# Three moves in a one-core graph network kernel: a late adjacency row, half of the turned features, and the queue of three outputs

## The chip, the core and the metric

The kernel runs on one core of one Trainium2 chip. The metric is the device time of one execution in microseconds. Before the change the median of three runs is 699.59 us (699.44 to 699.65).

The engines are called as in the profile: PE is TensorE (matmul), PEld its weight load, DVE is VectorE, ACT is ScalarE, POOL is GpSimd, SP is SyncE. SP, ACT and POOL also issue DMAs, each from a queue of its own that runs in program order.

## The reference

The input is `x` (3327 nodes, 64 features) and a symmetric-pattern, sparse adjacency matrix `adj` (3327 x 3327, f32, stored dense). Four layers, each with a layer norm and a relu in front and a residual (`x = x + layer(relu(norm(x)))`):

```python
# layer 0: twice h = relu(ggc(h, adj, ...)), a gated cell
m = adj @ (x @ W); gi = m @ wih.T + bih; gh = x @ whh.T + bhh
r, z = sigmoid(i_r + h_r), sigmoid(i_z + h_z); n = tanh(i_n + r * h_n)
h = (1 - z) * n + z * x
# layer 1: each row's last 100 neighbours, weighted by powers of 1/2
mask = adj != 0; rank = cumsum(mask, axis=1); k = min(deg, 100)
w = mask * where(rank > deg - k, 0.5 ** (deg - rank), 0); out = w @ (input @ weight) + bias
# layer 2: three times x = (adj * adj) @ x @ W.T + b
# layer 3: twice x = tanh(concat([adj @ x, x]) @ W)
```

So `adj` (or something made from it) is multiplied with a feature matrix eight times, one after the other.

## The kernel before, in words

**Tiles and stages.** The 3327 nodes are padded to 26 blocks of 128. The source nodes of a tile are one block q of 128; its columns are the target nodes of one of two groups. Group 0 has chunks 0 and 1 (3 and 3 blocks), group 1 has chunks 2 and 3 (3 and 4 blocks), each taken twice since two halves of the nodes (s = 0, 1) lie side by side. A tile is 128 x 2 x 768 f32 (group 0) or 128 x 2 x 896 (group 1), and is loaded by SP (L411) into one of 20 slots. The eight multiplications are numbered k = 0 to 7: 0 and 1 are layer 0, 2 is layer 1 ("ranked"), 3 to 5 are layer 2 ("squared": ACT, or DVE in part, squares the tile, L446 and L448), 6 and 7 are layer 3. A unit of work is (k, chunk, tile): two matmuls (L613), one for each s, into a PSUM bank that gathers the sums of a chunk over all 26 tiles. `alone` and `joint` list the units so that one loaded tile serves two multiplications of one group where it can. When a chunk's sums are complete, a task `after_k` turns them into the next features.

**The ranked stage.** A tile is first turned into a mask of ones and zeros (bf16). DVE compares with zero in two halves (L472), for 127 rows; the last row of the mask is not of the tile, but the count of neighbours that lie behind it, and comes by a small DMA on POOL's queue (L477) from `totals`. PE multiplies the mask with a triangle (L313), and ACT (L529) or DVE (L527) evicts the result with a relu as int16 bits, which read as bf16 are the powers of one half (`e`). PE multiplies those with the features (L613). A mask takes half a slot, called a room (class `Mask`). Since row 127 of every tile is left out, these "last sources" are gathered apart for each group by `last_sources(g)` (L564 to L583): POOL clears a room (L570), SP loads the rows 127 of all tiles into it (two DMAs, L574), DVE compares and scales (L576), subtracts the counts (L580), and ACT evicts (L582) into `lastw[g]`, which the last unit of the stage multiplies. The room is then free for a mask.

**Order.** The program is written out for each engine by hand; no scheduler changes the order. Tasks are Python generators: `yield us` says how much planned TensorE time must pass before the next step. `spend(us)` after each unit counts the planned time of that unit (0.86 us for a full unit) down for every task and runs those that are due. So the number in `later_task(200.0, ...)` and the yields inside a task decide where in each engine's program its instructions stand, and not when they run. `run` looks 44 units ahead for loads, 24 for masks, 3 for evictions; `mask_pieces` puts the halves of masks on DVE one or more at a time. `finish` runs the rest of a task at once, where its result is needed.

**What else the change touches.** `gru` (L874) is the gated cell of layer 0. Its sums are evicted into `both[c]`; ACT does the sigmoids (L890) and the tanh (L906), DVE the products (L895, L897, L910 to L912). For the first cell, the relu of one half of the features is made on DVE (L914, s = 1) and the other on ACT (L917, s = 0). Then `after_0` (L947) turns the features back to nodes on rows: for group 0 by matmuls with an identity, for group 1 by DVE's 32 x 32 transposes (L961), 8 for each s, into the tile that the matmuls of k = 1 read. `after_7` (L1029) is the end of the kernel for a chunk: sums evicted by ACT (L830) and DVE (L834), matmuls with the weights (L780), tanh on ACT (L1034), the residual on DVE (L1037), and the output by DMA on ACT's queue (L1039). Group 1's two chunks come out earlier; group 0 is last, with chunk 1 split into two parts (numbers 4 and 5), so that five outputs are issued in all.

Of the kernel before, what the change touches and what calls it, by code (L numbers as in the profile page):

```python
# [52 lines left out]
NC = 4  # L53
PARTS = (4, 5)
CWM = 512
GROUPS = [(0, 1), (2, 3)]
# [35 lines left out]
def upper(n):  # L92
    return slice(n * D, (n + 1) * D)
# [3 lines left out]
def kernel(  # L97
# [9 lines left out]
    nc = tc.nc  # L107
# [9 lines left out]
    xs = const.tile([P, NB, 2, D], F32, name="xs")  # L117
# [10 lines left out]
    both = [const.tile([P, 2, (b1 - b0) * P], F32, name=f"both{c}") for c, (b0, b1) in enumerate(CH[:NC])]  # L128
# [173 lines left out]
    def blocks(c):  # L302
        return CH[c][1] - CH[c][0]

    def width(c):
        return blocks(c) * P
# [15 lines left out]
    def take(sums=False, either=True):  # L322


        either = either and not sums
        pool = idle_sums if sums else idle_temps
        if either and idle_sums and (not pool or released[idle_sums[0]] < released[pool[0]]):
            pool = idle_sums
        for c in list(tasks):
            if not pool and c not in running:  # L330
                advance(c)
        i = pool.popleft()
        return i, banks[i]

    def give(i):
        released[i] = max(released) + 1
        (idle_sums if i < 4 else idle_temps).append(i)

    def nodes(c):

        return feat.tile([P, blocks(c), 2, D], F32, name=f"y{c}")

    def flat(t):
        return t.rearrange("p b s d -> p b (s d)")
# [4 lines left out]
    def xchunk(c):  # L349
        return xs[:, CH[c][0]:CH[c][1]]  # L350

    def view(ps, c):
        return ps[:, :width(c)].rearrange("p (b f) -> p b f", f=P)
# [5 lines left out]
    def advance(c):  # L359
        running.add(c)  # L360
        try:
            tasks[c][1] = next(tasks[c][0])
        except StopIteration:
            del tasks[c]
        running.discard(c)

    def begin(c, task):
        finish(c)
        tasks[c] = [task, 0.0]
        advance(c)  # L370

    def finish(c):
        while c in tasks:
            advance(c)

    def later_task(us, task):
        yield us
        yield from task
# [185 lines left out]
    def last_sources(g):  # L564

        w = sum(width(c) for c in GROUPS[g])
        w0 = CH[GROUPS[g][0]][0] * P
        room = Mask(w)
        v = room.view.rearrange("p s w -> p (s w)").bitcast(F32)
        nc.gpsimd.memset(v, 0.0)  # L570
        yield 4.0
        rows = adjT.rearrange("(q p) (s n) -> q p s n", p=P, s=2)
        for s in range(2):
            nc.sync.dma_start(out=v[s * D:s * D + NQ], in_=rows[:, P - 1, s, w0:w0 + w])  # L574
        yield 12.0
        nc.vector.tensor_scalar(v, v, 0.0, 129.0 * TWO7, op0=ALU.not_equal, op1=ALU.mult)  # L576
        for c in GROUPS[g]:
            finish(("count", c))
        yield 1.0
        nc.vector.scalar_tensor_tensor(v, totals[g], -TWO7, v, op0=ALU.mult, op1=ALU.add)  # L580
        yield 1.5
        nc.scalar.activation(lastw[g], v, AF.Relu, bias=bitsb)  # L582
        room.free()  # L583
# [189 lines left out]
    def stacked_to_nodes(c, w):  # L773

        i, ps = take()
        v = view(ps, c)
        for b in range(blocks(c)):
            for s in range(2):
                for n in range(2):
                    nc.tensor.matmul(v[upper(n), b, upper(s)], both[c][:, s, b * P + n * D:b * P + (n + 1) * D], w(s),  # L780
                                     start=True, stop=True)
        return i, v
# [46 lines left out]
    def evacuate_stacked(acc, c, on_scalar=False):  # L829
        nc.scalar.copy(both[c][upper(0), 0], acc[0][1][upper(0), :width(c)])  # L830
        if on_scalar:
            nc.scalar.copy(both[c][upper(1), 1], acc[1][1][upper(1), :width(c)])
        else:
            nc.vector.tensor_copy(both[c][upper(1), 1], acc[1][1][upper(1), :width(c)])  # L834
        for i in {acc[0][0], acc[1][0]}:
            give(i)
# [31 lines left out]
    def add_row(c, i):  # L868
# [2 lines left out]
        nc.vector.tensor_tensor(groups(xchunk(c)), groups(xchunk(c)),  # L871
                                brow[:, i:i + 1, :].to_broadcast([P, n, D]), ALU.add)

    def gru(acc, c, bi, bh, cell, pace=1.0):  # L874

        w = width(c)
        evacuate_stacked(acc, c, on_scalar=cell == 0)
        yield 0.8 * pace
        at = dead.popleft()
        r, z, d = (slots[at].rearrange("p s w -> p (s w)")[:, i * CWM:i * CWM + w] for i in range(3))  # L880

        def gate(g):
            i, ps = take()
            for s in range(2):
                nc.tensor.matmul(ps[upper(1 - s), :w], cells[:, cell, s, g, :], both[c][:, s], start=True, stop=True)  # L885
            return i, ps

        for g, v in enumerate((r, z)):
            i, ps = gate(g)
            nc.scalar.activation(v, ps[:, :w], AF.Sigmoid, bias=bsum[:, cell, g:g + 1])  # L890
            give(i)
        nh = None if cell == 0 else gate(2)
        ni = gate(3)
        yield 1.0 * pace
        nc.vector.scalar_tensor_tensor(r, ahead[c] if nh is None else nh[1][:, :w], bcol[:, bh + 2:bh + 3], r,  # L895
                                       op0=ALU.add, op1=ALU.mult)
        nc.vector.tensor_tensor(r, r, ni[1][:, :w], ALU.add)  # L897
        give(ni[0])
        if nh is not None:
            give(nh[0])  # L900
        else:
            del ahead[c]
            if not any(ch in ahead for ch in GROUPS[c // 2]):
                rooms[c // 2].free()
        yield 1.0 * pace
        nc.scalar.activation(r, r, AF.Tanh, bias=bcol[:, bi + 2:bi + 3])  # L906
        yield 0.8 * pace
        for s in range(2):
            u = upper(1 - s)
            nc.vector.tensor_tensor(d[u], both[c][u, s], r[u], ALU.subtract)  # L910
        nc.vector.tensor_tensor(d, d, z, ALU.mult)
        nc.vector.tensor_tensor(d, d, r, ALU.add)  # L912
        if cell == 0:
            nc.vector.tensor_scalar(both[c][upper(0), 1], d[upper(0)], 0.0, None, op0=ALU.max)  # L914
        yield 2.4 * pace
        if cell == 0:
            nc.scalar.activation(both[c][upper(1), 0], d[upper(1)], AF.Relu)  # L917
            yield 1.0 * pace
        return at, d
# [27 lines left out]
    def after_0(c, acc):  # L947
        at, _ = yield from gru(acc, c, BI1, BH1, 0)
        dead.append(at)
        yk = nodes(c)  # L950
        if c in GROUPS[0]:
            i, v = stacked_to_nodes(c, lambda s: ident[:, upper(1 - s)])
            yield 0.8
            nc.vector.tensor_copy(flat(yk), v)
            give(i)
        else:
            for s in range(2):
                v = both[c][upper(1 - s), s].rearrange("p (b q n) -> p b q n", q=4, n=32)
                for f in range(2):
                    for q in range(4):  # L960
                        nc.vector.transpose(yk[q * 32:(q + 1) * 32, :, s, f * 32:(f + 1) * 32],  # L961
                                            v[f * 32:(f + 1) * 32, :, q])
                    yield 0.6
        y[1][c] = yk

    def after_1(c, acc):
        pace = 1.0 if c in GROUPS[0] else 1.2
        at, h2T = yield from gru(acc, c, BI2, BH2, 1, pace)
        v = transpose_to_nodes(h2T, c)
        dead.append(at)  # L970
        yield 0.8 * pace
        residual(v, c, relu=True)
        yk = nodes(c)
        yield from layernorm_relu(yk, c, TWO27, 1.2 * pace, squares_on_scalar=c in GROUPS[1])
        y[2][c] = yield from in_three(yk, c)
        yield 80.0 if c in GROUPS[1] else 14.0
        add_row(c, 3)
# [51 lines left out]
    def after_7(c, acc):  # L1029
        evacuate_stacked(acc, c)  # L1030
        yield 1.3
        v = stacked_to_nodes(c, lambda s: w3[:, 1, s])
        t = work.tile([P, 4, 2, D], F32, name="t2")[:, :blocks(c)]
        nc.scalar.activation(flat(t), v[1], AF.Tanh)  # L1034
        give(v[0])
        yield 0.8
        nc.vector.tensor_tensor(flat(xchunk(c)), flat(xchunk(c)), flat(t), ALU.add)  # L1037
        g0, g1 = CH[c]
        nc.scalar.dma_start(out=out[:, g0:g1], in_=xs[:, g0:g1])  # L1039

    after[:] = [after_0, after_1, after_2, after_3, after_4, after_5, after_6, after_7]

# [20 lines left out]
    begin(2, later_task(4.0, before_0(2)))  # L1063
    begin(3, later_task(10.0, before_0(3)))
    begin(NC + 1, later_task(130.0, last_sources(0)))
    begin(NC + 2, later_task(200.0, last_sources(1)))
    run()
    for c in list(tasks):
        finish(c)
# [39 lines left out]
```

## Time and profile before

| | before |
|---|---|
| runs, median (lowest to highest) | 699.59 us (699.44 to 699.65) |
| profiled execution | 699.51 us |
| its span on the core | 697.6 us |
| granted TensorE clock | 0.999 |
| PE busy | 680.2 us, 97% |
| DVE, ACT, POOL busy | 354.5, 274.4, 79.1 us |
| L613, the multiplications with f32 tiles | 535.5 us in 3016 matmuls |
| L961, transposes of layer 0 for group 1 | 9.1 us in 32 |
| L576, L580, L582, for both groups | 1.2, 2.0 and 2.0 us in 2 each |
| L1037, the last residuals | 2.5 us in 5 |

The profile's times are microseconds from the start of the span. A timeline row gives the start, the busy time, engine, line and operation, what is written `<-` what is read, the count of instructions in the row, and in brackets the idle time of the engine ahead of it with what ended it. `SPq`, `ACTq` and `POOLq` are the issue of DMAs on that engine. [...]

### The profile page before, as it was taken

Reading aid. Unit: us, or ns where it says so; the run is one execution under the profiler, and the core shown is the slowest. Engines: PE = TensorE matmul, PEld = TensorE weight load, DVE = VectorE, ACT = ScalarE, POOL = GpSimd, SP = SyncE. Lnnn points to the kernel's source line nnn. Section 1 sums busy time; section 2 is a strip of 40 time slices with the busy share of each in tenths; the row PEclk is TensorE's granted clock in tenths of the full one; section 3 lists DMA queues with packets and bytes.
Section 4 is the critical chain, followed back from the end, with each engine's and each line's share of the span. In section 5 each row is a group of like instructions: output and inputs, shape, how many; then the busy total and the mean of one; then the engine's idle time right before and its main releaser. Section 6 shows DMA issues by size and latency. Waiting matters only on the chain.

```text
span 697.6 us, 12581 instructions
## 1 busy us (share of the span) xinstructions
PE 680.2 (97%) x5072; PEld 377.9 (54%) x5072; DVE 354.5 (51%) x772; ACT 274.4 (39%) x426; POOL 79.1 (11%) x114
## 2 busy tenths in 40 slices
PE   6899999999999998999999999999999999999997
PEld 4686667635566785556444444333344444344586
DVE  5946745665997899747442107325271565005101
ACT  1013000403147878888998107722176500000101
POOL 5300000002390423111100000000000000000000
PEclk9999999999999999999999999999999999999999
DMA  9999998099879534783899569954998399918991
GB/s 339 401 401 406 405 406 268 3 359 377 268 246 369 212 126 153 267 276 121 288 382 330 203 222 408 405 217 141 394 367 269 105 402 405 405 59 285 403 403 45
DMA packets 68693, 201.31 MB, mean 289 GB/s; under 512 B 7244, under 2 KB 8372, under 8 KB 68636
## 3 DMA queue, kind: packets, MB, share of 16 engines
q1 hardware_dynamic: 65292, 198.69, 76.5%
q10 hardware_dynamic: 1168, 1.63, 0.7%
q8 instruction: 40, 0.66, 0.4%
q0 software_dynamic: 2176, 0.20, 0.2%
q14 instruction: 17, 0.14, 0.1%
HBM read 199.45 MB, written 0.85 MB: 287 GB/s over the span
## 4 chain that ended last, share of the span: by engine, by line
PE 86%; DVE 8%; DMA 3%; POOL 2%; issue 1%; ACT 1%; ACTq 0%; DVEq 0%; POOLq 0%
PE sum L613 73%; PE temp L313 5%; DMA adj<-in_adjT 2%; PE temp L548 2%; PE temp L885 2%; DVE adj L472 2%; PE sum L313 1%; PE sum L885 1%; PE temp L780 1%; DVE e L527 1%; DVE adj L910 1%; POOL both L251 1%; DVE y L961 1%; POOL st L854 1%; DVE st L851 1%
## 5 line engine op out<-in xcount | busy, mean ns | idle before, releaser
L613 PE MATMUL sum<-adj,y 128*64 128x384 f32 (+3 forms) x3016 | 535.5, 501 | 4.0 <-DVE y L858 1.4
L613 PEld LDWEIGHTS sum<-adj,y 128*64 128x64 f32 x3016 | 248.0, 137 | 233.8 <-issue 197.9
L446 ACT ACTIVATE adj<-adj 128x768 f32<-128x768 f32 (+1 forms) x176 | 144.3, 892 | 45.7 <-PE sum L613 21.9
L472 DVE TENSOR_SCALAR adj<-adj 128x768 bf16<-128x768 f32 (+3 forms) x208 | 113.4, 596 | 32.6 <-PE temp L548 24.7
L613 PE MATMUL sum<-e,both 128*64 128x384 bf16 (+1 forms) x624 | 73.9, 339 | 1.1 <-DVE e L527 1.1
L529 ACT ACTIVATE e<-temp,bitsb 128x384 int16<-128x384 f32 (+1 forms) x120 | 67.6, 608 | 14.7 <-PE temp L313 9.4
L830 ACT COPY both<-sum 64x384 f32<-64x384 f32 (+3 forms) x17 | 8.1, 478 | 149.0 <-PE sum L613 147.9
L854 POOL TENSOR_TENSOR st<-st,mhalf 128x6 f32<-128x6 f32 (+1 forms) x16 | 24.9, 1554 | 288.7 <-DVE st L852 288.7
L834 DVE COPY both<-sum 64x384 f32<-64x384 f32 (+3 forms) x13 | 7.2, 560 | 98.6 <-ACT both L830 98.6
L448 DVE TENSOR_TENSOR adj<-adj 128x768 f32<-128x768 f32 (+1 forms) x32 | 30.6, 1005 | 51.8 <-DMA adj<-in_adjT 33.1
L613 PEld LDWEIGHTS <-both 128*64 128x64 bf16 x624 | 41.2, 110 | 19.6 <-issue 7.0
L313 PE MATMUL temp<-adj,tri 128*64 128x384 bf16 (+1 forms) x332 | 51.4, 341 | 0.4 <-DVE e L527 0.2
L477 POOL DMA_DIRECT2D adj<-totals x52 | 34.8, 671 | 46.3 <-PE temp L313 32.4
L527 DVE TENSOR_SCALAR e<-temp 128x384 int16<-128x384 f32 (+1 forms) x46 | 28.3, 616 | 20.6 <-ACT e L529 10.9
L313 PEld LDWEIGHTS <-tri 128*64 128x64 bf16 x416 | 28.9, 110 | 16.1 <-issue 7.8
L809 DVE STREAM_TRANSPOSE both<-y 32x96 f32<-32x96 f32 (+1 forms) x128 | 35.6, 278 | 2.9
L548 PE MATMUL temp<-adj,behind 128*64 128x384 bf16 x208 | 33.8, 340 | 2.6 <-DVE adj L472 2.5
L825 DVE STREAM_TRANSPOSE y<-t 32x96 f32<-32x96 f32 (+1 forms) x64 | 17.8, 278 | 24.7 <-ACT t L816 23.9
L548 PEld LDWEIGHTS <-behind 128*64 128x64 bf16 x208 | 20.8, 110 | 17.2 <-issue 13.3
L761 DVE COPY t<-sum 128x384 f32<-128x384 f32 x6 | 3.3, 553 | 35.8 <-PE sum L613 35.8
L186 ACT COPY t<-temp 128x128 f32<-128x128 f32 x1 | 0.3, 266 | 48.2 <-PE temp L184 48.2
L570 POOL MEMSET adj<- 128x768 f32 (+1 forms) x2 | 1.6, 790 | 139.4 <-PE sum L613 133.9
(132 smaller groups left out, 352.0 us busy)
## 6 DMA issues: line engine op xcount, KB each, us to landing
adj<-in_adjT SPq DMA_DIRECT2D x130, 768.0 KB, 9.1
adj<-in_adjT SPq DMA_DIRECT2D x104, 896.0 KB, 11.6
xs<-in_x ACTq DMA_DIRECT2D x1, 448.0 KB
adj<-totals POOLq DMA_DIRECT2D x26, 3.0 KB, 4.9
adj<-totals POOLq DMA_DIRECT2D x26, 3.5 KB, 2.5
out<-xs ACTq DMA_DIRECT2D x2, 192.0 KB, 4.4
out<-xs ACTq DMA_DIRECT2D x1, 256.0 KB
xs<-in_x ACTq DMA_DIRECT2D x1, 192.0 KB, 3.4
```

Source lines behind the costliest of these rows:

```text
L313: nc.tensor.matmul(out[hs], lhsT[:, hs], rhs, start=start, stop=stop)
L446: nc.scalar.activation(sq, v, AF.Square)
L448: nc.vector.tensor_tensor(sq, v, v, ALU.mult)
L472: nc.vector.tensor_scalar(t.mask.view[:rows, half], t.view()[:rows, half], 0.0, None, op0=ALU.not_equal)
L477: nc.gpsimd.dma_start(out=t.mask.view[P - 1:P], in_=totals[t.g][t.q:t.q + D + 1:D, :])
L527: nc.vector.tensor_scalar(wide[:, s], ps[:, :w], BITS, 0.0, op0=ALU.add, op1=ALU.max)
L529: nc.scalar.activation(wide[:, s], ps[:, :w], AF.Relu, bias=bitsb)
L548: nc.tensor.matmul(counts[c][1][s * D:(s + 1) * D, :w], behind[:, NQ - 1 - t.q:NQ - 1 - t.q + D], t.mask.view[:, s, t.cols(c)], start=firs ...
L613: nc.tensor.matmul(acc[h][1][h * D:(h + 1) * D, :w], yq[h], rhs[h], start=first and n == 0, stop=last and n == len(terms) - 1)
L809: nc.vector.transpose(to[at:at + 32, :, q], h[q * 32:(q + 1) * 32, :, s, f * 32:(f + 1) * 32])
L854: nc.gpsimd.tensor_tensor(st[:, 3, :n], st[:, 2, :n], mhalf[:, :n], ALU.pow)
L885: nc.tensor.matmul(ps[upper(1 - s), :w], cells[:, cell, s, g, :], both[c][:, s], start=True, stop=True)
```

## The change

Three things are edited.

First, the transposes of group 1's features after k = 0. A helper `turn` makes the 8 transposes of one s. `gru` calls it for s = 1 right behind DVE's relu, before it yields; `after_0` calls it for s = 0 where all 16 stood, and the yields of 0.6 between them are gone.

Second, `last_sources(1)` begins after 240 us of planned time and not 200. In the program of the engines this puts POOL's L570 fifteen places further on in its queue, directly behind the mask row that is issued at 296.06 in the profile of before; SP's two L574 ten loads later; DVE's L576 and L580 and ACT's L582 close to the end of group 1's ranked stage. The rooms of the masks made in between are handed out in another order, and the last mask of the stage is made in the room that L582 frees. The order of PE's instructions is the same.

Third, the outputs of chunks 0 and 1 (three DMAs: chunk 0, parts 4 and 5) are issued on SP's queue. Those of group 1 stay on ACT's.

```diff
+    turned = {}
+
+    def turn(yk, c, s):
+
+        v = both[c][upper(1 - s), s].rearrange("p (b q n) -> p b q n", q=4, n=32)
+        for f in range(2):
+            for q in range(4):
+                nc.vector.transpose(yk[q * 32:(q + 1) * 32, :, s, f * 32:(f + 1) * 32], v[f * 32:(f + 1) * 32, :, q])
+
     def gru(acc, c, bi, bh, cell, pace=1.0):
...
             nc.vector.tensor_scalar(both[c][upper(0), 1], d[upper(0)], 0.0, None, op0=ALU.max)
+            if c in GROUPS[1]:
+                turned[c] = nodes(c)
+                turn(turned[c], c, 1)
         yield 2.4 * pace
...
     def after_0(c, acc):
         at, _ = yield from gru(acc, c, BI1, BH1, 0)
         dead.append(at)
-        yk = nodes(c)
         if c in GROUPS[0]:
+            yk = nodes(c)
...
         else:
-            for s in range(2):
-                v = both[c][upper(1 - s), s].rearrange("p (b q n) -> p b q n", q=4, n=32)
-                for f in range(2):
-                    for q in range(4):
-                        nc.vector.transpose(yk[q * 32:(q + 1) * 32, :, s, f * 32:(f + 1) * 32],
-                                            v[f * 32:(f + 1) * 32, :, q])
-                    yield 0.6
+            yk = turned.pop(c)
+            turn(yk, c, 0)
         y[1][c] = yk
...
-        nc.scalar.dma_start(out=out[:, g0:g1], in_=xs[:, g0:g1])
+        queue = nc.scalar if c in GROUPS[1] else nc.sync
+        queue.dma_start(out=out[:, g0:g1], in_=xs[:, g0:g1])
...
-    begin(NC + 2, later_task(200.0, last_sources(1)))
+    begin(NC + 2, later_task(240.0, last_sources(1)))
```

## Prediction, made before the changed kernel ran

> **What bounds the kernel now.** I first read the page's totals and its chain of waits.
>
> ```profile
> span 697.6 us, 12581 instructions
> PE 680.2 (97%) x5072; PEld 377.9 (54%) x5072; DVE 354.5 (51%) x772; ACT 274.4 (39%) x426; POOL 79.1 (11%) x114
> PE 86%; DVE 8%; DMA 3%; POOL 2%; issue 1%; ACT 1%; ACTq 0%; DVEq 0%; POOLq 0%
> ```
>
> TensorE is busy 680.2 of 697.6 us. The change takes no work from it, so a gain can only come out of the 17.4 us in which it stands. Next, the windows of 5 us (columns: wall, busy PE, PEld, DVE, ACT, POOL, clock, DMA share, GB/s) show where it stands near the edits.
>
> ```profile
> 145.00:150.00 5.00, 4.28 (x25) 1.61 (x24) 4.74 (x17) 0.00 (x0) 0.00 (x0) 1.00 0.81 278
> 270.00:275.00 5.00, 4.30 (x45) 2.82 (x43) 5.00 (x11) 4.85 (x8) 3.29 (x4) 1.00 0.26 45
> 275.00:280.00 5.00, 3.20 (x23) 1.41 (x21) 5.00 (x9) 3.99 (x5) 0.48 (x1) 1.00 0.43 166
> 315.00:320.00 5.00, 5.00 (x58) 3.17 (x56) 4.78 (x9) 4.62 (x9) 2.19 (x4) 1.00 0.05 14
> 690.00:695.00 5.00, 3.28 (x61) 2.87 (x55) 1.78 (x5) 1.78 (x5) 0.00 (x0) 1.00 0.14 46
> ```
>
> At 145 and at 270 to 280 PE waits while VectorE is full: there VectorE is the bound. At 315 to 320 PE is full, and VectorE and ScalarE nearly are. At 690 the chain of the outputs is all that is left. The timelines of these places give what ends each wait.
>
> [...] when DMA is idle: the mask rows of L477 land 1.6 us after issue at 317 to 320, but 5 us among loads (285.88 to 291.01); 6.4 is the longest. [...]
>
> **Part A, the turned features (L957 to L963).** The first 8 transposes of chunk 2 need only VectorE's own relu (s=1), the other 8 need ScalarE's (L917); now they stand in one block behind the latter.
>
> ```profile
> 132.79 0.35 DVE L914 TENSOR_SCALAR both<-adj 64x384 f32<-64x384 f32 x1
> 136.12 0.75 DVE L895 SCALAR_TENSOR_TENSOR adj<-adj,bcol,adj 128x512 f32<-128x512 f32 x1 [2.98 <-ACT adj L890]
> 138.38 2.25 DVE L961 STREAM_TRANSPOSE y<-both 32x96 f32<-32x96 f32 x8 [0.58 <-ACT both L917]
> 143.88 7.33 DVE L961 STREAM_TRANSPOSE y<-both 32x96 f32<-32x96 f32 x24
> 146.17 1.29 PE L613 MATMUL sum<-adj,y 128*64 128x384 f32 x6 [0.72 <-DVE y L961]
> ```
>
> Eight of width 96 take 2.25 us, and VectorE idles 2.98 us at 133.1. So the s=1 half of chunk 2 goes there for nothing (133.2 to 135.4, before L895 at 136.12). The s=0 half stays at 138.38. Behind 143.9 only chunk 3's 16 are left, 7.33 − 2.25 = 5.1 us, ending near 149.0. PE's matmuls on s=1 of chunk 2 then don't wait at 146.17. The half unit before starts at 144.83, and its successors follow each 0.43 us, so 145.26 was due: **0.9 us** gained (0.72 of it shown as idle). Next late is chunk 3's features: PE asks for them at 150.73 now, 149.8 then; 149.0 is 0.8 us early. Without the idle place the 2.25 us would come back at L895. Loads have 14 us or more of slack in this stage. Bounds: 0.7 to 1.0.
>
> **Part B, group 1's last sources (L564 to L583).** Seven instructions move: L570, two L574, L576, L580, L582 and the waits with them. First what they leave.
>
> ```profile
> 274.87 0.61 DVE L576 TENSOR_SCALAR adj<-adj 128x896 f32<-128x896 f32 x1
> 275.40 0.68 DVE L527 TENSOR_SCALAR e<-sum 128x512 int16<-128x512 f32 x1
> 276.00 1.15 DVE L472 TENSOR_SCALAR adj<-adj 127x896 bf16<-127x896 f32 x2
> 277.07 1.08 DVE L580 SCALAR_TENSOR_TENSOR adj<-totals,adj 128x896 f32<-128x896 bf16 x1
> 278.61 0.55 DVE L527 TENSOR_SCALAR e<-sum 128x384 int16<-128x384 f32 x1
> 279.21 1.08 PE L613 MATMUL sum<-adj,y 128*64 128x512 f32 x4 [1.19 <-DVE e L527]
> ```
>
> VectorE runs without a gap, and PE waits for L527. By starts, L576 takes 0.53 us of that row and L580 1.00. Without them the L527 at 278.61 is done at 277.63 and PE goes on at 277.68 instead of 279.21; its own work is ready at 277.15. **1.53 us** gained. ScalarE's L582 (1.04 us at 278.19) leaves as well, and counts nothing, since VectorE is the later one. Bounds: 1.2 (another wait takes the end of it) to 1.6.
>
> On SP and POOL:
>
> ```profile
> SPq L574 <- POOL adj L570: 23.2, 2, 22.0
> POOL adj L477 <- ACT lastw L582: 5.9, 1, 5.9
> ```
>
> SP stands 22.0 us (231.7 to 253.8) at L574 and the loads behind it land by 260; the first mask of them is made at 279.68. Unblocking them is worth nothing, as they are early already. At the new place L574 stands behind L570, and that behind the mask row of 296.06 on POOL: memset near 296.6, both L574 near 297.5 to 298.6 (0.54 each). The load behind them went out at 297.34: 1.3 us late, against 8 us between its landing (304.3) and its mask. Nothing.
>
> Now what they enter. By the order of instructions L576, one L472, one L527 and L580 stand among the last masks of group 1 (VectorE, 316 to 319), and L582 on ScalarE between evictions (L529) that run 13 in 6.42 us without a gap from 317.64, in the time of before at about 319.5. Two things follow.
> - The evictions behind L582 come 0.95 us later; they had 0.2 to 0.5 us in hand, so TensorE waits about 0.7 us.
> - The last mask is made in the half slot that L582 frees: its L472 and its row by DMA (L477, POOL) wait for L582, which ends at 320.58. Before, that room was free, and the last three rows were issued at 317.19 to 318.30, one behind the other. A row issued at 320.62 lands 1.6 us later as at 317.19, or 2.45 as the one that followed L582 before (279.52 to 281.97): 322.2 to 323.1. PE starts on that mask (L313) at 321.59. Wait 0.6 to 1.5 us. VectorE's own 1.5 us more bring the mask's halves to about 321.7, no later than that.
>
> The two lie over one another, so the larger counts: **1.1 us** lost, taken between 0.7 and 1.5. Bounds: 0 (if spare evictions and the row come in time) to 5.4 (row at 6.4 us). Behind it, lastw is wanted at 325.16 only, and no load hangs on it.
>
> **Part C, group 0's outputs (L1039).** Three issues go from ScalarE's queue to SP's.
>
> ```profile
> 691.34 0.34 ACTq L1039 DMA_DIRECT2D out<-xs  x1
> 691.72 0.76 ACT L830 COPY both<-sum 64x256 f32<-64x256 f32 x2 [1.00 <-DVE xs L1037]
> 693.21 0.38 ACT L1034 ACTIVATE t<-temp 128x256 f32<-128x256 f32 x1 [0.73 <-PE temp L780]
> 694.53 0.28 ACT L1034 ACTIVATE t<-temp 128x128 f32<-128x128 f32 x1 [0.93 <-DVE xs L1037]
> ```
>
> ScalarE stands at the first issue until VectorE's L1037 ends (691.31), with L830 of the next part queued behind it, whose sums are done near 691.05. Then the same for the last part: L1034 at 694.53 is behind an issue that waits for L1037 (694.06). Through SP: L830 at 691.05, L834 ends 691.85, PE's L780 straight behind the last L613 (692.1 to 692.9), L1034 at 692.95 and 693.35, L1037 until 693.8 and 694.1, issues from 693.8 and 694.15. SP's issue of a load takes 0.54 us, ScalarE's 0.34: the last ends at 694.5 to 694.7, against 695.5 now. **0.9 us** gained (0.8 to 1.0). SP has issued its last load at 668.7, so nothing is in front of them; next late is VectorE's L1037 of the last part.
>
> **Sum.** Against the profiled execution of 699.51 us (span 697.6 and 1.9 around it; the median of the runs, 699.59, is 0.08 away, which I leave): 699.51 − 0.9 − 1.53 − 0.9 + 1.1 = 697.3 us. Within 0.2% of 699.59 (698.2 to 701.0) a measurement can hardly tell it from no change.
>
> **Rivals.**
> - *The last mask costs nothing* (row and evictions in time): 697.3 − 1.1 = 696.2. For it speaks 4.2 us without DMA at 320; against it that L582's end is later than the old issue by 2.3 us. Chance 0.14.
> - *The gains are given back*: a PE that is 2.4 us earlier from 279 meets masks or loads that are not earlier (from 285 to 312 rows take 5 us and masks hang on them); A and half of B1 vanish, 697.3 + 0.9 + 0.75 = 698.9. For it: VectorE is full from 253 to 281. Against it: what releases loads and masks there is PE itself, which moves along. Chance 0.2.
> - *Slower: the last row is late.* The mechanism is L477 behind L582 alone, at 320.6. With the longest landing of this trace, 6.4 us, PE stands 320.62 + 6.4 − 321.59 = 5.4 us, and the time is 699.51 − 3.33 + 5.4 = 701.6. It turns to a loss from a landing of 4.3 us on, and to a clear one from 5.7. For it: rows at 285 to 311 took 3.4 to 5.4. Against it: DMA is at 0.05 and 0.01 of its rate at 315 to 325, and rows took 1.6 there. Chance 0.08.
> - *Part C does not do what it says*: SP's issue and landing eat the gain, 697.3 + 0.9 = 698.2, on the bound. Chance 0.08.
>
> **The numbers.** Forecast 0.5, with 696.7 to 698.0 from the bounds of its terms. Faster by over 0.2%: 0.5 + 0.14 + half of the last rival = 0.68; same: 0.2 + 0.04 = 0.24; slower 0.08. The range reaches from the first rival with C and A at their upper bounds (696.2 − 0.2, and 0.3 for what B's eviction may add: 695.7) to a row that takes 4.4 us (699.5), which takes in the second rival.
>
> **What would show it.** A: eight L961 at 133, no L961 wait of PE at 146. B: no L576 or L580 at 275, PE back before 278; L582 near 317 in the new time, a PE wait of about 1 us for the last mask's row or an L529, and L574's wait gone from SP at 231. C: the three out issues on SP, L830 near 1 us earlier against the last L613, the span's tail 0.9 us shorter behind PE's last matmul. I am wrong if PE's idle time near 320 is over 2 us, or the 2.4 us don't reach from 281 to 315.

## The result, and the profile after

The changed kernel takes 697.73 us (median; 697.54 to 698.06) against 699.59 before (699.44 to 699.72). The ratio is 0.9974, with a 95% interval of 0.9963 to 0.9984: 1.9 us less. The profiled execution took 697.73 us with a span of 695.7.

TensorE has the same 5072 matmuls in the same order in both programs, so the clearest reading is the start of the same matmul in both traces. I call the difference the lead (start before minus start after). The last column is the end of the last matmul of all; the median is of the timed runs.

| matmul that started before at | 120.1 | 160.2 | 265.2 | 300.1 | 330.2 | 691.5 | end of the last | median us |
|---|---|---|---|---|---|---|---|---|
| the change | -0.06 | 0.89 | 0.88 | 2.43 | 1.00 | 0.98 | 1.30 | 697.73 |

The lead changes in three steps: +0.95 at part A, +1.55 at 276 to 279, -1.43 at 319 to 322. Between 120 and 691.5 nothing else moves by more than 0.1 us. From there to the end of the span the tail is another 0.9 us shorter (1.9 in the span, less the lead of 0.98).

The windows of after that answer to those shown of before (their columns are the same):

```profile
145.00:150.00 5.00, 5.00 (x30) 2.18 (x28) 3.94 (x13) 0.00 (x0) 0.00 (x0) 1.00 0.78 276
270.00:275.00 5.00, 4.22 (x42) 2.57 (x40) 5.00 (x10) 4.48 (x8) 3.21 (x5) 1.00 0.03 6
275.00:280.00 5.00, 4.81 (x41) 2.42 (x39) 4.16 (x9) 3.73 (x6) 0.54 (x1) 1.00 0.13 22
315.00:320.00 5.00, 4.70 (x50) 2.67 (x46) 4.32 (x7) 4.81 (x11) 1.29 (x2) 1.00 0.02 4
320.00:325.00 5.00, 4.41 (x50) 3.53 (x52) 1.99 (x4) 4.09 (x8) 0.00 (x0) 1.00 0.00 1
690.00:695.00 5.00, 2.10 (x49) 1.96 (x44) 1.67 (x5) 1.23 (x4) 0.00 (x0) 0.93 0.25 82
```

TensorE is full at 145 and nearly so at 275 to 280. It now stands in part at 315 to 325, where it was full before: the window of before at 315 is shown above, and this is the next one.

```profile
320.00:325.00 5.00, 5.00 (x62) 3.40 (x60) 2.61 (x5) 4.75 (x10) 0.00 (x0) 1.00 0.01 3
```

**Part A.** The timeline of VectorE, and one row of TensorE's:

```profile
133.24 2.24 DVE L881 STREAM_TRANSPOSE y<-both 32x96 f32<-32x96 f32 x8
136.19 0.75 DVE L904 SCALAR_TENSOR_TENSOR adj<-adj,bcol,adj 128x512 f32<-128x512 f32 x1 [0.70 <-ACT adj L899]
144.06 5.05 DVE L881 STREAM_TRANSPOSE y<-both 32x128 f32<-32x128 f32 x16
142.65 4.70 PE L613 MATMUL sum<-adj,y 128*64 128x384 f32 x24
```

Eight transposes (now L881) lie in what was an idle 2.98 us; 0.70 are left. The 16 of chunk 3 end at 149.11, and the first matmul on them starts at 149.84. TensorE's row runs through with 24 matmuls and no wait.

**Part B, what it leaves.** VectorE and TensorE at the place where L576 and L580 stood:

```profile
276.18 0.54 DVE L527 TENSOR_SCALAR e<-sum 128x384 int16<-128x384 f32 x1
276.77 1.08 PE L613 MATMUL sum<-adj,y 128*64 128x512 f32 x4 [0.19 <-DVE e L527]
```

The wait for this L527 was 1.19 us and is 0.19.

**Part B, what it enters.** ScalarE, POOL and TensorE near the last mask of group 1, and below them a row of the answer on line 313 between 317 and 322 (durations in ns, min/median/max, then first and last start):

```profile
317.11 1.04 ACT L582 ACTIVATE lastw<-adj,bitsb 128x896 int16<-128x896 f32 x1
318.44 0.99 POOL L477 DMA_DIRECT2D adj<-totals  x1 [3.15 <-ACT lastw L582]
318.67 0.82 PE L313 MATMUL temp<-adj,tri 128*64 128x384 bf16 x4 [0.16 <-ACT e L529]
320.59 0.52 PE L313 MATMUL temp<-adj,tri 128*64 128x384 bf16 x4 [0.61 <-ACT e L529]
```

```profile
L313 PEldq EVENT_SEMAPHORE  x3: 51/51/1262, 317.3 to 319.3; - x3
```

The timeline puts the wait at 320.59 down to an eviction on ScalarE. But the wait of 1262 ns in the second fence is TensorE's sequencer, which stands from 319.27 to 320.53 ahead of the weight load of that same L313; that wait carries the DMA of the mask's row, which landed at 320.50. An eviction happened to end at 320.51, which is why the timeline names it; the one that this L313 needs had ended at 319.56. Which of the two it was is for the experiments.

**Part C.** ScalarE's and SP's tail:

```profile
690.11 0.37 ACT L830 COPY both<-sum 64x256 f32<-64x256 f32 x1 [0.38 <-PE sum L613]
691.24 0.26 ACT L830 COPY both<-sum 64x128 f32<-64x128 f32 x1 [0.77 <-PE sum L613]
691.88 0.61 ACT L1041 ACTIVATE t<-temp 128x256 f32<-128x256 f32 x2 [0.38 <-PE temp L780]
690.35 3.24 SPq L1047 DMA_DIRECT2D out<-xs  x3
```

ScalarE waits for TensorE only, no more for VectorE, and the two tanh (now L1041) are back to back. The three issues on SP take 0.37 to 0.39 us each; the last one ends at 693.59 and lands at 694.79, against 696.71 before.

### The profile page after: what moved, and what is told of

It reads as the page before. It is cut to its first block, busy times and chain, and to the rows that moved or that the text cites. A ratio compares the mean times of both kernels' runs of the same rounds, so it can differ in the third digit from the quotient of the medians.

```text
span 695.7 us, 12589 instructions
## 1 busy us (share of the span) xinstructions
PE 681.0 (98%) x5072; PEld 380.4 (55%) x5072; DVE 355.3 (51%) x772; ACT 274.3 (39%) x426; POOL 77.8 (11%) x114
## 4 chain that ended last, share of the span: by engine, by line
PE 58%; DVE 1%; ACT 0%; POOL 0%; issue 0%; DVEq 0%; ACTq 0%; POOLq 0%
PE sum L613 54%; PE temp L313 3%; PE temp L780 1%; ACT e L529 0%; POOL st L854 0%; DVE both L834 0%; DVE e L527 0%; PE sum L313 0%; ACT both L830 0%; DVE y L858 0%; DVE y L850 0%; DVE t L845 0%; DVE st L851 0%; DVE st L843 0%; DVE xs L865 0%
## 5 line engine op out<-in xcount | busy, mean ns | idle before, releaser
L472 DVE TENSOR_SCALAR adj<-adj 128x768 bf16<-128x768 f32 (+3 forms) x208 | 114.0, 597 | 32.6 <-PE temp L548 24.7
L830 ACT COPY both<-sum 64x384 f32<-64x384 f32 (+3 forms) x17 | 8.1, 478 | 148.2 <-PE sum L613 148.2
L313 PE MATMUL temp<-adj,tri 128*64 128x384 bf16 (+1 forms) x332 | 51.7, 341 | 1.3 <-ACT e L529 0.8
L313 PEld LDWEIGHTS <-tri 128*64 128x64 bf16 x416 | 29.2, 110 | 17.3 <-issue 9.8
L527 DVE TENSOR_SCALAR e<-temp 128x384 int16<-128x384 f32 (+1 forms) x46 | 28.3, 615 | 20.0 <-PE temp L313 9.6
L570 POOL MEMSET adj<- 128x768 f32 (+1 forms) x2 | 1.6, 800 | 133.2 <-PE sum L613 133.2
```

What stands on the lines that cost most here:

```text
L313: nc.tensor.matmul(out[hs], lhsT[:, hs], rhs, start=start, stop=stop)
L472: nc.vector.tensor_scalar(t.mask.view[:rows, half], t.view()[:rows, half], 0.0, None, op0=ALU.not_equal)
L527: nc.vector.tensor_scalar(wide[:, s], ps[:, :w], BITS, 0.0, op0=ALU.add, op1=ALU.max)
```

## Experiments

My theory after the result: three independent parts; B is a gain on VectorE and a smaller loss at the last mask of group 1, which the row of that mask sets, with the evictions behind L582 underneath it. All leads read as in the table above.

| kernel | 120.1 | 160.2 | 265.2 | 300.1 | 330.2 | 691.5 | end of the last | median us |
|---|---|---|---|---|---|---|---|---|
| turned features only | -0.08 | 0.89 | 0.87 | 0.89 | 0.89 | 0.89 | 0.89 | 698.68 |
| last sources only | -0.12 | -0.13 | -0.11 | 1.44 | 0.00 | -0.02 | -0.02 | 699.60 |
| outputs only | -0.01 | -0.01 | 0.01 | 0.02 | 0.02 | 0.02 | 0.34 | 698.55 |
| room kept | -0.55 | 0.40 | 0.40 | 1.97 | 1.20 | 1.18 | 1.50 | 697.56 |
| begun at 210 | -0.23 | 0.73 | 0.73 | 1.91 | 1.91 | 1.93 | 2.24 | 696.45 |
| begun at 250 | 0.12 | 1.08 | 1.02 | 2.57 | 2.32 | 2.30 | 2.62 | 696.60 |
| one output on SP | -0.03 | 0.93 | 0.93 | 2.48 | 1.05 | 1.03 | 1.35 | 698.27 |
| early load | -0.02 | 0.94 | 0.94 | 2.48 | 1.05 | 1.03 | 1.35 | 697.55 |
| the change again | -0.12 | 0.84 | 0.83 | 2.38 | 0.95 | 0.92 | 1.24 | 697.71 |
| room kept again | -0.16 | 0.81 | 0.79 | 2.34 | 1.57 | 1.56 | 1.87 | 697.13 |
| lastw on VectorE | -0.02 | 0.94 | 0.93 | 2.50 | 0.64 | 0.62 | 0.93 | 698.37 |
| last row on SP | -0.11 | 0.85 | 0.81 | 2.36 | 1.56 | 1.54 | 1.86 | 697.51 |

### Each part alone

The kernel before, with one part of the diff each: the helper `turn` and its two calls; or `later_task(240.0, last_sources(1))`; or the queue of the outputs.

> Part A alone (half of the turned features behind VectorE's relu), the rest as before. Theory: PE's matmuls on the s=1 features of chunk 2 start 0.9 us earlier than at 146.17, and this lead is kept to the end: about 698.7 us, 0.9 below before. Rival (the lead is given back to masks or loads later): the matmuls near 281 or 321 start no earlier than before, and the time is 699.6 us.

> Part B alone (group 1's last sources at 240), the rest as before. Theory: PE leads by 1.6 us at 279.2 and loses 1.4 us of it at the last mask of group 1 (318 to 321.6), so the time is about 699.4 us, hardly different from before: the two halves of part B nearly cancel. Rival (the loss near 320 in the full change came from PE being early by part A as well, so that it shrinks without A): the loss is 0.5 us or less and the time is 698.5 us.

> Part C alone (group 0's outputs on SP's queue), the rest as before. Theory: PE runs as before up to its last matmul of L613; behind it the tail is 0.9 us shorter: 698.7 us. Rival (part of that 0.9 us belongs to the other parts): 699.2 us or more.

Measured: 698.68 us (ratio 0.9985, 0.9978 to 0.9992), 699.60 (0.9998, 0.9989 to 1.0006) and 698.55 (0.9986, 0.9979 to 0.9993). By medians that is 0.9, 0.0 and 1.0 us less than the 699.55 of the kernel before in these runs, and 1.8 together, where the change gives 1.9. So the parts don't touch each other by more than 0.1 us. Part A's 0.89 is kept to the last matmul; it is not given back. What of it the idle place does, and what the yields that are gone do, was not run apart. Part B leads by 1.44 at 300 and by nothing at 330: alone it is worth nothing. TensorE being early by part A is not what causes the loss, since it is the same without A.

### Where the loss near 320 is from

First, the last mask in another half slot. The room is given back later, for group 1 only:

```diff
         nc.scalar.activation(lastw[g], v, AF.Relu, bias=bitsb)
+        if g:
+            yield 6.0
         room.free()
```

> The full change, but the room of the last sources is given back 6 us of planned time later, so that the last mask of group 1 is made in another half slot and its row by DMA waits no more for the eviction L582 on ScalarE. L582 stays where it is. Theory (the row of the last mask costs the last 0.8 us of the loss near 320, the evictions behind L582 the first 0.6): PE leads before by about 1.8 us instead of 1.0 behind 321.6, and the time is 696.9 us. Rival (the evictions alone set the loss, and the row came in time): the lead stays at 1.0 us, 697.7 us.

Measured: 697.56 us (ratio 0.9965, 0.9952 to 0.9978), so by its time a miss. Its trace shows a loss near 320 of 1.97 - 1.20 = 0.77 us instead of 1.43, as expected, but also a lead that is 0.5 us smaller at 120 already, where the two kernels have the same instructions. Is this chance, or are the 0.65 us given back? I ran both once more, side by side.

> The changed kernel itself once more, beside the next one on the same chip, since the room kept gave 697.56 us where 696.9 was expected, while its trace showed the expected 0.65 us near 320 and a loss of 0.5 us at 58 us, where the two kernels are the same. Both theories: 697.7 us.

> The kernel with the room kept once more. Theory (the wait at 58 us is chance, the 0.65 us of the row are real): 0.6 us under the changed kernel of the same call, about 697.0 us. Rival (the gain near 320 is given back elsewhere): the same time as the changed kernel within 0.2 us.

Measured: 697.71 us and 697.13 us (ratios to before 0.9975, 0.9965 to 0.9984, and 0.9965, 0.9951 to 0.9979), 0.6 us apart. Leads at 120 are alike now (-0.12 and -0.16), and the losses near 320 are 1.43 and 0.77. The 0.5 us were the first trace's own. With the room kept, the last two rows (timeline of POOL) are issued one behind the other, well ahead of L582:

```profile
314.85 1.07 POOL L477 DMA_DIRECT2D adj<-totals  x2 [1.35 <-PE temp L313]
```

So 0.66 us of the loss are the row's, and 0.77 stay when it is early. Next, the other half: `lastw` evicted by VectorE, so that ScalarE's evictions aren't held.

```diff
-        nc.scalar.activation(lastw[g], v, AF.Relu, bias=bitsb)
+        if g:
+            nc.vector.tensor_scalar(lastw[g], v, BITS, 0.0, op0=ALU.add, op1=ALU.max)
+        else:
+            nc.scalar.activation(lastw[g], v, AF.Relu, bias=bitsb)
```

> The full change, but group 1's lastw is evicted by VectorE (add and max in one tensor_scalar, as L527 does it) and not by ScalarE, at the same place; the last mask's room and row wait for that. Theory (two causes that lie over one another: evictions held by L582, and the row): PE's waits of 0.3 us each at 318.7 and 319.1 are gone, but the row is issued no earlier than before (near 318.4, as VectorE has two masks ahead of it) and lands near 320.4, so PE waits there 1.2 us at once and the lead behind it is about 1.2 us: 697.5 us. Rival (ScalarE's evictions were all of it): loss 0.3 us or less, 696.5 us.

Measured: 698.37 us (0.9983, 0.9976 to 0.9989), slower than the change, and 0.9 us above what I expected. The loss near 320 is 2.50 - 0.64 = 1.86 us instead of 1.2 or so, most of it in one wait (timelines of VectorE, POOL and TensorE):

```profile
317.47 0.62 DVE L583 TENSOR_SCALAR lastw<-adj 128x896 int16<-128x896 f32 x1
318.39 1.41 POOL L477 DMA_DIRECT2D adj<-totals  x1 [3.16 <-DVE lastw L583]
320.95 0.52 PE L313 MATMUL temp<-adj,tri 128*64 128x384 bf16 x4 [1.43 <-ACT e L529]
```

The rival is out: with ScalarE free of L582, the loss is larger, not smaller. The row goes out at 318.39 as expected, but its issue takes 1.41 us and not 0.54, and it lands at 320.86. That is the part that I had wrong. Here too the timeline names an eviction for the wait, and the row's landing fits it (320.86, start at 320.95).

Why is the issue so long? Where few loads or none run beside it, the row lands 1.05 to 1.07 us after its issue has ended in each of these cases: 0.54 and 0.58 us of issue before at 317 to 318, 0.99 in the change, 1.40 before at 279.52, 1.41 here. The long ones lie beside two or three L472 on VectorE, and end 0.1 us after one of those has ended. My guess from these rows was that L472 holds GpSimd's issue up, and that an issue on SP would be shorter. So the last row alone from SP's queue:

```diff
+    rows_of = [0, 0]
...
+                rows_of[t.g] += 1
+                queue = nc.sync if t.g and rows_of[1] == NQ else nc.gpsimd
-                nc.gpsimd.dma_start(out=t.mask.view[P - 1:P], in_=totals[t.g][t.q:t.q + D + 1:D, :])
+                queue.dma_start(out=t.mask.view[P - 1:P], in_=totals[t.g][t.q:t.q + D + 1:D, :])
```

> The full change, but the row of the last mask of group 1 alone is issued on SP's queue and not on GpSimd's; it waits for L582 as before. Two loads behind it on SP go out near 319 instead of 305 and 308, and are wanted by ScalarE near 335. Theory (GpSimd's issue of that row is long, 0.99 us against 0.54, because VectorE runs L472 beside it, and the row lands 1.06 us after the end of the issue): SP issues it in 0.4 us from 318.2 and it lands by 319.8 to 320.1; of the loss of 1.4 us 0.8 to 1.1 remain, 697.2 to 697.4 us. Rival (the time from issue to landing is the transfer's own, and the same from any queue): the row lands at 320.5 and the time is 697.7 us.

Measured: the loss near 320 is 2.36 - 1.56 = 0.80 us, nearly that of the room kept (0.77). TensorE's sequencer stood 629 ns for the row and not 1262, so it came about 0.6 us earlier after nearly the same lead. SP's issue took 0.60 us, where I had expected 0.4. The time is 697.51 us (0.9971, 0.9960 to 0.9981), 0.1 us above the expected range though. The trace has the reason at the very end: SP's last instructions wait for the DMA semaphores one after the other, some 0.06 us each, and one more DMA on SP has turned the order, so that the last output's comes early and seven more follow it. From the last landing (694.23) to the end of the span are 1.3 us here, against 0.9 in the change (694.79 to 695.7).

By itself this run can't tell an issue that VectorE holds up from a queue that is quicker anyway. The issues of all rows on GpSimd can: the 14 traces of this document hold 727 of them (much the same 52 in each). For every one I looked up how long after its start the next compare with zero (L472 or L576) began on VectorE.

| the compare began, after the issue did | issues | of these over 0.72 us |
|---|---|---|
| 0.09 to 0.29 us | 103 | 103 (0.74 to 1.41 us) |
| 0.30 to 0.32 us | 99 | 73 (0.94 to 0.96 us) |
| later | 525 | 0 (0.71 us at most) |

Each of the 176 long issues ended 0.09 to 0.10 us after such a compare had ended. Evictions out of PSUM (L527) and instructions with two inputs that began 0.05 to 0.29 us after the issue, with no compare there, left it at 0.59 us or less. So in these traces the issue was long where a compare began 0.09 to 0.29 us into it, in part where it began at 0.30 to 0.32 us, and never where it began later; by what means one holds up the other, no view shows. The row at 317.73 of before, issued beside L472 in 0.58 us, is no counterexample: one L472 had begun 0.13 us before the issue and ended 0.48 us after its start, and the next began at 0.40. In the change the hold is built in, since the two halves of the last mask and its row all wait for L582. The halves are the last two of these five on VectorE, and the second began at 318.72, 0.28 us after the issue of the row:

```profile
316.47 2.87 DVE L472 TENSOR_SCALAR adj<-adj 127x896 bf16<-127x896 f32 x5
```

### The same work at other times

`later_task(210.0, ...)` and `later_task(250.0, ...)` in place of 240, all else as in the change.

> The full change, but group 1's last sources begin at 210 of planned time and not 240. L576, L580 and L582 then stand behind the crowded stretch of VectorE (its end is near 279 to 281) and ahead of 290, where ScalarE's evictions have 1.2 to 1.9 us in hand by the trace of the changed kernel, and the freed room goes to a load and to no mask. Theory (the gain is what VectorE no longer does at 275, the loss is what ScalarE and the last row do near 320, and both depend only on the place): PE leads before by 2.4 us from 280 on and keeps it at 321.6; 696.3 us. Rival (the three instructions cost wherever they are put, as TensorE is full): a loss of 0.9 us or more again, 697.2 us or above.

> The full change, but group 1's last sources begin at 250 of planned time, 10 later. L582 then stands behind the train of evictions, no mask takes the freed room, and only the last unit of the stage (at 325 in the time of before) waits for it. Theory (the loss near 320 is L582 inside the train plus the row behind it): the loss of 1.4 us shrinks to 0.4 us or less, lead about 2.1 us behind 326, 696.6 us. Rival (VectorE's 1.7 us near 316 to 319 are what is late): the loss stays at 1 us or more, 697.3 us or above.

Measured: 696.45 us (0.9956, 0.9943 to 0.9968) and 696.60 us (0.9958, 0.9945 to 0.9972), both better than the change by 1.1 to 1.3 us. At 210 nothing is lost from 300 to 691.5 (1.91, 1.91, 1.93); 0.4 us of the gain at 265 to 300 are missing (1.18 instead of 1.55). At 250 the loss is 0.25 us. ScalarE's timelines show where L582 is now, of the first kernel and of the second:

```profile
286.38 1.03 ACT L582 ACTIVATE lastw<-adj,bitsb 128x896 int16<-128x896 f32 x1
```

```profile
320.68 1.10 ACT L582 ACTIVATE lastw<-adj,bitsb 128x896 int16<-128x896 f32 x1
```

The first stands where ScalarE had idle time (0.56 us ahead of each of the evictions at 282.51 and 285.90), the second behind the full train (12 evictions from 315.06 to 320.85), with no mask waiting for its room. The rival at 210 is out: the three instructions don't cost wherever they are put. The rival at 250 is not tested by that run as it should be, since VectorE's L576 and L580 have moved with L582 (to 318.77 and 319.42, behind the last masks). That they aren't what is late in the change is read from its own trace: the last half of the last mask ended at 319.34 (316.47 and 2.87 above), and the row landed at 320.50.

The trace of the kernel at 210 also shows where its missing 0.4 us are. L570, by which GpSimd clears the room, now runs beside an L472 in the stretch where VectorE is full:

```profile
263.75 0.86 POOL L570 MEMSET adj<- 128x896 f32 x1
264.08 1.01 DVE L472 TENSOR_SCALAR adj<-adj 127x896 bf16<-127x896 f32 x1
```

In the change the same L472 (at 263.94) took 0.65 us. VectorE is 0.4 us later from there on, and TensorE waits 0.80 us for its L527 at 268.60, where it waited 0.43 in the change. No run moved L570 alone.

Then the loads L574 at their old place, with only the arithmetic moved (begun at 200, and `yield 52.0 if g else 12.0` ahead of L576):

> The full change, but room, memset (L570) and the two loads L574 stay where they were before the change (begun at 200), and only L576, L580 and L582 are moved to where the change has them. SP then stands some 22 us at L574 again. Theory (that stand costs nothing, all of the gain is VectorE's): the same as the full change, 697.7 us, with PE leading by 2.4 us at 281 and by 1.0 us at 322. Rival (part of the gain comes from SP no longer standing there): PE leads by 1.9 us or less at 281, 698.2 us or more.

Measured: 697.55 us (0.9969, 0.9958 to 0.9980), with the leads of the change, 2.48 and 1.05. SP stands at L574 as before:

```profile
SPq L574 <- POOL adj L570: 23.2, 2, 22.0
```

So these 22 us cost nothing, and taking them away gave nothing.

### One output of three on SP

```diff
-        queue = nc.scalar if c in GROUPS[1] else nc.sync
+        queue = nc.sync if c == 0 else nc.scalar
```

> The full change, but only chunk 0's output is issued on SP; parts 4 and 5 go out on ScalarE as before. Theory (two waits of ScalarE behind an issue, one each): L830 of part 4 is early as in the full change, but L1034 of part 5 stands again behind the issue of part 4, some 0.7 us later than in the full change; the issue itself is 0.2 us shorter on ScalarE. 0.5 us over the full change, 698.2 us. Rival (only the first wait matters, the tail is then the last transfer): no difference, 697.7 us.

Measured: 698.27 us (0.9981, 0.9974 to 0.9989), 0.5 us over the change. ScalarE:

```profile
692.70 0.34 ACTq L1047 DMA_DIRECT2D out<-xs  x1
693.14 0.28 ACT L1041 ACTIVATE t<-temp 128x128 f32<-128x128 f32 x1 [0.93 <-DVE xs L1044]
```

The last tanh stands 0.93 us behind part 4's issue again, as it did before. So about half of part C's 0.9 us is L830 being early, and the other half is this.

## Why the prediction was right, point by point

- *Part A, 0.9 us.* Right: 0.95 of lead in the change, 0.97 alone. The cover was where it was said (133.2), chunk 3's transposes ended at 149.1 against 149.0 worked out, and were wanted at 149.84. The loads gave nothing back.
- *Part B, what it leaves, 1.53 us.* Right: 1.54 to 1.57 in every kernel with the last sources at 240 or 250, with or without the other parts. That SP's 22 us are worth nothing was right as well (early load).
- *Part B, what it enters, 1.1 us.* The mechanism was right, the size was off: 1.43 us. "The two lie over one another, so the larger counts" holds: evictions alone 0.77 (worked out 0.7), the row 1.43 in all (worked out 0.6 to 1.5). I took a value between them, where the row's upper end was due. The term that was too small is the row's landing: L582 ended where I had it (318.15 plus the lead of 2.44 is 320.59, against 320.58), but the row went out 0.3 us behind that, and its issue took 0.99 us and not 0.54. The sum has the row go out 0.04 us behind L582, while the trace of before has 0.29 (279.23 to 279.52). The 2.45 us of the row at 279.52, which I had as the slow end, was such a held issue (1.40 us), and the trace showed its duration beside it.
- *Part C, 0.9 us.* Right: 0.9 in the change, 1.0 alone by medians. SP's issues took 0.37 to 0.39 us, not the 0.54 of a load; the last ended at 693.59, which with the lead of 0.98 is 694.57, inside the 694.5 to 694.7.
- *Sum.* 697.3 forecast, 697.73 measured: 0.33 of the difference is the row. The gains of A, B and C were together 0.1 larger than worked out, the start of the span was 0.06 later, and 2.0 us of the profiled execution lay outside the span, not 1.9. One price was misread without effect: the two L574 were put at 0.54 us each, while those of the trace of before took 0.72 together (253.81).
- *Rivals.* "The last mask costs nothing" is refuted by the lead at 330 (1.00), and "the gains are given back" by the lead at 300, where all of 2.43 is still there. "The last row is late" names the right wait; it would have needed a landing of over 4.3 us, and took 2.06. "Part C does not do what it says" is out.

## What to carry to other kernels

A step moved out of a crowded place is worth what it frees there less what it does where it lands, and the second part is read like the first: how much each queue has in hand at the new place, and who takes the buffer that it gives back. Here that buffer went to the last mask of the stage, and the same step 30 of planned time earlier or 10 later gave 1.1 to 1.3 us more. Where a wait is on several semaphores, don't take the timeline's name for it: look at the sequencer's own wait, and take one of the candidates away.

## What the runs showed of the hardware that I had not expected

- GpSimd's issue of a row of 3 or 3.5 KB took 0.54 us mostly, but 0.74 to 1.41 us in all 103 cases where a compare of VectorE (L472 or L576) began 0.09 to 0.29 us after it, and it then ended 0.1 us after such a compare. In the cases above with few loads or none beside it, the row landed 1.05 to 1.07 us after the issue's end, after an issue of 0.54 us as after one of 1.41.
- The other way round, one L472 took 1.01 us (at 264.08, begun at 210) while GpSimd cleared a room (L570) beside it, and 0.65 us in the change without that.
- The time from the last landing to the end of the span was 0.9 us in the change, where SP asks for the last output's DMA semaphore last, and 1.3 us with the last row on SP, where it asks for seven more behind it, some 0.06 us each.
